# Cross-attention on one core: weights turned on VectorE for TensorE tiles of 32x32, products chained in PSUM, divisions on GpSimd

## The chip, the cores and the metric

The kernel runs on one core of one Trainium2 chip. The metric is the device time of one execution in microseconds (us); lower is better. A core has five engines with a queue each: TensorE (PE, matrix products into PSUM; PEld is its loading of weights), VectorE (DVE), ScalarE (ACT), GpSimd (POOL) and SyncE (SP), which here only issues DMAs. Every engine works through its own queue in order and waits for others by semaphores.

## What is computed

A block of an image model on x of shape (8, 512, 512): a cross-attention with a residual ("x" in the names of the tiles), a self-attention ("a"), a second cross-attention ("c") and an MLP ("m"). All is fp32. The part that matters is the cross-attention, which is there twice. With B = 8, N = 512 rows, H = 512 channels, 16 heads of 32 and a context of S = 77 rows:

```python
q = (xq @ Wq + bq).reshape(B, Lq, nh, dh)
kv = (xkv @ Wkv + bkv).reshape(B, Lkv, 2, nh, dh)
k = kv[:, :, 0]
v = kv[:, :, 1]
scores = jnp.einsum('bqhd,bkhd->bhqk', q, k) / jnp.sqrt(jnp.float32(dh))
attn = jax.nn.softmax(scores, axis=-1)
out = jnp.einsum('bhqk,bkhd->bqhd', attn, v).reshape(B, Lq, H)
return x_q + (out @ Wp + bp)
```

`xq` and `xkv` are layer-normalised (and in the first one modulated) rows of x and of the context.

## The kernel before

`cross_phase` (from L537) runs one cross-attention. Keys `kT` and values `vs` of all batches are made beforehand; `vs` holds the values with the 77 context rows on partitions and is loaded once from DRAM (L394, L466). The loop at L786 has B x KC = 32 rounds, one for each batch `b` and each group `fc` of four heads (128 channels). Four rounds are called a block here.

A round computes the scores of its own group and carries, between them, the rest of the group before (`before`) and a piece of the projections of neighbouring batches:

- `Softmax.scores` (L681): 16 products (L687) of 128 query rows by 77 context rows, contraction 32, four heads side by side in the array. They go to two PSUM tiles `sc[0]`, `sc[1]` of two banks each, from the pool `ps_s` with two such tiles. Half 0 gets its maxima (L703), a subtraction (L704) and one exponential (L714); half 1 gets negated maxima (L710) and eight exponentials of 77 columns (L717) with the maxima as bias.
- `total` (L724) sums the weights, `divide` (L727, L728) takes the reciprocal and multiplies; all on VectorE.
- `turn` (L741) turns the weights of one head with four products by the identity into PSUM; `keep` (L745) copies them to SBUF on ScalarE. There are four pairs a round.
- `outputs` (L751): four products, contraction 77, of 32 channels by 512 rows, in four column tiles of the array; ScalarE reads them with the value bias (L759).
- One `Seven` (L486) in each round in the middle of the stage: seven half-size products (L509) for a 2x2 split of a 512-wide product, for queries (`queries`, L610) or for the output projection (`project`, L641). Each product is two matmuls over K. Products 1, 6, 2, 5, 7, 4, 3 go to halves of PSUM banks of the pool `ps_m`; p1, u2, p5, u3, u4 are the intermediate sums that VectorE, ScalarE and GpSimd make. Queries are made at fc = 0 and 3, projections at fc = 1 and 2.
- `ln_rows` (L251) normalises the rows of a coming batch in pieces, `turned_rows` (L763) turns them with four groups of transposes (L280) and four ScalarE evictions (L284); this is in the round fc = 2. `x_sums` and `o_sums` (L590, L600) make the sums that the seven products need, four GpSimd instructions each.

The order of the instructions on TensorE, VectorE, ScalarE and GpSimd is the order of the Python code, by `manual_schedule`; nothing is reordered. A wait at the head of a queue therefore holds all behind it.

Of the kernel before, what the change touches and what calls it, by code (L numbers as in the profile page):

```python
# [19 lines left out]
P = 128  # L20
# [9 lines left out]
def tile_pixart_block(ctx: ExitStack, tc: tile.TileContext, a: dict, out: bass.AP):  # L30
# [241 lines left out]
    def ln_T(b, nm, pool, psp, res, scale=None, shift=None, tag="t"):  # L272


        xb = x_sb[nm, b]
        xT = res["xT"] = pool.tile([P, KC, N], F32, tag="xnT", bufs=1, name=f"xnT_{nm}{b}")
        for k in range(KC):
            pt = psp.tile([P, H], F32, tag=tag, name=f"lnT_ps_{nm}{b}_{k}")
            for t in range(NT):
                nc.tensor.transpose(pt[:, ts(t, P)], xb[:, t, ts(k, P)], ident)  # L280
            if scale is None:
                nc.scalar.copy(xT[:, k, :], pt)
            else:
                nc.scalar.activation(  # L284
                    xT[:, k, :], pt, AF.Identity,
                    bias=shift[:, k, b : b + 1], scale=scale[:, k, b : b + 1],
                )
            yield
# [49 lines left out]
    with tc.tile_pool(name="ps_s", bufs=2, space=PSUM, reuse_waits="tile") as ps_s:  # L338
# [17 lines left out]
        def context_x(eps, w_k, w_v, bkv, work, prep, cx):  # L356
# [3 lines left out]
            vs = work.tile([S, B, H], F32, tag="cv", bufs=1, name="cv_x")  # L360
# [33 lines left out]
            nc.sync.dma_start(out=vs, in_=vd.rearrange("(b s) h -> s b h", s=S))  # L394
# [13 lines left out]
            return kT, vs, last, mark, mv  # L408

        class ContextC:  # L410
# [42 lines left out]
            def room(self, pool):  # L453
                self.kT = pool.tile([P, KC, R], F32, tag="ckT", bufs=1, name="ckT_c")
                self.vs = pool.tile([S, B, H], F32, tag="cv", bufs=1, name="cv_c")

            def values(self, t):
# [7 lines left out]
                if t == CT - 1:  # L465
                    nc.sync.dma_start(out=self.vs, in_=self.vd.rearrange("(b s) h -> s b h", s=S))  # L466
# [19 lines left out]
        class Seven:  # L486
# [5 lines left out]
            ORDER = (1, 2, 6, 5, 7, 4, 3)  # L492

            def __init__(self, nm, lhs, rhs, work, first, fifth, third, dst, done=None):
                self.nm, self.lhs, self.rhs, self.work = nm, lhs, rhs, work
                self.first, self.fifth, self.third = first, fifth, third
                self.dst, self.done = dst, done

            def temp(self, tag):
                return self.work.tile([P, N2], F32, tag=tag, bufs=1 + (tag != "u3"), name=f"{tag}_{self.nm}")  # L500

            def steps(self):
                add = ALU.add
                for n, i in enumerate(self.ORDER):
                    if n % 2 == 0:
                        bank = ps_m.tile([P, 2, N2], F32, tag="m", name=f"s{n}_ps_{self.nm}")
                    ps = bank[:, n % 2]
                    for k in range(2):
                        nc.tensor.matmul(  # L509
                            ps, lhsT=self.lhs[i][:, k], rhs=self.rhs[i][:, k],  # L510
                            start=(k == 0), stop=(k == 1),
                        )

                    if i == 2:
                        p1 = self.temp("p1")
                        self.first(p1, bank[:, 0])
                        nc.vector.tensor_tensor(self.dst[0, 0], ps, p1, add)
                    elif i == 5:
                        u2, p5 = self.temp("u2"), self.temp("p5")
                        nc.vector.tensor_tensor(u2, bank[:, 0], p1, add)  # L520
                        self.fifth(p5, ps)
                        u4 = self.temp("u4")
                        nc.gpsimd.tensor_tensor(u4, u2, p5, add)
                    elif i == 4:
                        u3 = self.temp("u3")
                        self.third(u3, bank[:, 0], u2)
                        nc.gpsimd.tensor_tensor(self.dst[1, 1], u3, p5, add)
                        nc.vector.tensor_tensor(self.dst[1, 0], ps, u3, add)
                        if self.done is not None:
                            self.done(1)  # L530
                    elif i == 3:
                        nc.vector.tensor_tensor(self.dst[0, 1], ps, u4, add)
                        if self.done is not None:
                            self.done(0)
                    yield

        def cross_phase(  # L537
            nm, eps, w, names, modulated, kT, vs, stack, behind, following, head, fill
# [10 lines left out]
            add, sub = ALU.add, ALU.subtract  # L549

# [3 lines left out]
            def sums(engine, s1, s2, s3, s4, a11, a12, a21, a22):  # L554

                engine.tensor_tensor(s1, a21, a22, add)
                engine.tensor_tensor(s2, s1, a11, sub)
                engine.tensor_tensor(s3, a11, a21, sub)
                engine.tensor_tensor(s4, a12, s2, sub)

            def differences(engine, t1, t2, t3, t4, b11, b12, b21, b22):

                engine.tensor_tensor(t1, b12, b11, sub)
                engine.tensor_tensor(t2, b22, t1, sub)
                engine.tensor_tensor(t3, b22, b12, sub)
                engine.tensor_tensor(t4, b21, t2, sub)
# [4 lines left out]
            sums(  # L571
                nc.gpsimd, *sq,
                w_q[:, low, :H2], w_q[:, high, :H2], w_q[:, low, H2:], w_q[:, high, H2:],
            )
            to = four("to", [P, 2, H2])

            dq = small.tile([P, 2], F32, tag="dq", bufs=1, name=f"dq_{nm}")
            nc.vector.tensor_tensor(dq, bias_cols(bq, 2, 2), bias_cols(bq, 2, 0), sub)


            db = work.tile([P, H2], F32, tag="db", bufs=1, name=f"db_{nm}")
            nc.gpsimd.tensor_tensor(db, bo_row[:, H2:], bo_row[:, :H2], sub)

            def weights_o():
                differences(
                    nc.gpsimd, *to,
                    w_o[:, low, :H2], w_o[:, low, H2:], w_o[:, high, :H2], w_o[:, high, H2:],
                )

            def x_sums(b, engine):  # L590
# [4 lines left out]
                differences(  # L595
# [4 lines left out]
            def o_sums(b, engine):  # L600
# [4 lines left out]
                sums(  # L605
# [4 lines left out]
            def queries(b, j):  # L610
# [7 lines left out]
                for i in range(2):  # L618
# [8 lines left out]
                }  # L627
                return Seven(
                    f"q{nm}{b}_{j}", lhs, rhs, work,

                    lambda p1, ps: nc.scalar.activation(
                        p1, ps, AF.Identity, bias=bias_cols(bq, 1, j)
                    ),
                    lambda p5, ps: nc.scalar.copy(p5, ps),
                    lambda u3, ps, u2: nc.vector.scalar_tensor_tensor(
                        u3, ps, dq[:, j : j + 1], u2, add, add
                    ),
                    {(r, c): qT[r][:, (first, second)[c]] for r in range(2) for c in range(2)},
                ).steps()

            def project(b, j):  # L641
# [16 lines left out]
                def fifth(p5, ps):  # L658
                    nc.scalar.copy(p5, ps)
                    nc.gpsimd.tensor_tensor(p5, p5, db, add)  # L660

                def done(r):
# [6 lines left out]
                    f"o{nm}{b}_{j}", lhs, rhs, work,  # L669
                    lambda p1, ps: nc.vector.tensor_tensor(p1, ps, bo_row[:, :H2], add), fifth,  # L670
                    lambda u3, ps, u2: nc.vector.tensor_tensor(u3, ps, u2, add),
                    {(r, c): res[j + 2 * r][:, ts(c, H2)] for r in range(2) for c in range(2)}, done,
                ).steps()

            class Softmax:


                def __init__(self, b, fc):
                    self.b, self.fc, self.nm = b, fc, f"{nm}{b}_{fc}"

                def scores(self, before):  # L681
                    b, fc = self.b, self.fc
                    qT = st[b]["q"].pop(fc)
                    sc = [ps_s.tile([P, 2, H], F32, tag="s", name=f"s_{self.nm}_{i}") for i in range(2)]
                    for t in range(NT):
# [12 lines left out]
                    self.p = [  # L698
                        work.tile([P, 2, NT, S], F32, tag="p", bufs=4, name=f"p_{self.nm}_{i}")
                        for i in range(2)  # L700
                    ]

                    nc.vector.tensor_reduce(self.mx[0], self.sv[0], AX.X, ALU.max)  # L703
                    nc.vector.tensor_tensor(  # L704
                        self.p[0], self.sv[0], self.mx[0].unsqueeze(3).to_broadcast([P, 2, NT, S]),
                        ALU.subtract,
                    )
                    if before:
                        before.divide(1)
                    nc.vector.tensor_reduce(self.mx[1], self.sv[1], AX.X, ALU.max, negate=True)  # L710

                def exp(self, i, r=0):
                    if i == 0:
                        nc.scalar.activation(self.p[0], self.p[0], AF.Exp)  # L714
                        return
                    for t in range(NT):
                        nc.scalar.activation(  # L717
                            self.p[i][:, r, t, :], self.sv[i][:, r, t, :], AF.Exp,
# [3 lines left out]
                def total(self, i):  # L722
                    self.sm = small.tile([P, 2, NT], F32, tag="sums", name=f"sm_{self.nm}_{i}")
                    return nc.vector.tensor_reduce(self.sm, self.p[i], AX.X, ALU.add)  # L724

                def divide(self, i):
                    nc.vector.reciprocal(self.sm, self.sm)  # L727
                    return nc.vector.tensor_tensor(  # L728
                        self.p[i], self.p[i], self.sm.unsqueeze(3).to_broadcast([P, 2, NT, S]), ALU.mult
                    )  # L730

                def turn(self, h):

                    if h == 0:
                        self.pT = [
                            work.tile([S, 2, H], F32, tag="pT", bufs=2, name=f"pT_{self.nm}_{i}")
                            for i in range(2)
                        ]
# [887 lines left out]
```

## Time and profile before

| | us |
|---|---|
| median of 3 runs | 2536.84 |
| lowest, highest | 2528.83, 2537.41 |
| span of the profiled execution | 2534.4 |
| first scores to the next stage's first transposes, x | 81.6 to 453.4 |
| the same, c | 1364.8 to 1725.1 |

The span is measured from the first to the last instruction of the profiled execution. Busy times in the profile are sums over instructions that can overlap on TensorE; the clock column of a stretch is the share of full speed that TensorE was granted. The page's row of TensorE clock over 40 equal slices:

```profile
PEclk9899999999999999999999999999999999999999
```

Chains of waits give start and length of each piece in us; groups of instructions give the count, the busy time in us and the mean in ns.

### The profile page before, as it was taken

The page shows a single profiled execution, that of the slowest core. Times are in us where ns is not written, and L with a number is a line of the kernel's source. Part 1 is how long each engine was busy: PE and PEld are TensorE (multiplying, and loading weights), DVE is VectorE, ACT ScalarE, POOL GpSimd, SP SyncE. Part 2 cuts the span into 40 slices and gives each one's busy share as a digit, 9 for nine tenths or more (in the row PEclk, how much of TensorE's full clock was granted, in tenths as well). Part 3 has the DMA queues.
Part 4 walks back from the last instruction along what each step waited for, and adds up shares of the span by engine and source line. Part 5 has one row for each costly group of instructions (what it writes and reads, how often), then busy time and mean ns, then how long its engine had stood idle before and what let it go on. Part 6 is the DMA issues. An engine that isn't in the chain of part 4 may idle for free.

```text
span 2534.4 us, 35276 instructions
## 1 busy us (share of the span) xinstructions
PE 2433.2 (96%) x13205; PEld 1561.7 (62%) x13205; DVE 1776.2 (70%) x3230; ACT 1226.2 (48%) x2083; POOL 1087.0 (43%) x982
## 2 busy tenths in 40 slices
PE   7999999889999999999989999998999999999998
PEld 3577776423333333333335777767888888888887
DVE  3588887478889888887756888877556555555553
ACT  1466665377677777777653666662121121121120
POOL 2245452266767777767663454535102102012011
PEclk9899999999999999999999999999999999999999
DMA  7323313498989999999996223133111111001010
GB/s 261 137 51 92 92 26 76 90 180 168 199 171 197 191 181 186 182 188 180 201 200 173 68 39 63 19 81 82 40 32 38 33 39 38 26 29 55 17 38 25
DMA packets 112068, 265.05 MB, mean 105 GB/s; under 512 B 12210, under 2 KB 28674, under 8 KB 111770
## 3 DMA queue, kind: packets, MB, share of 16 engines
q0 software_dynamic: 50976, 159.45, 35.1%
q1 hardware_dynamic: 54981, 91.59, 10.9%
q10 hardware_dynamic: 5941, 11.76, 1.4%
q8 instruction: 104, 1.70, 0.3%
q14 instruction: 66, 0.54, 0.1%
HBM read 226.39 MB, written 44.76 MB: 107 GB/s over the span
## 4 chain that ended last, share of the span: by engine, by line
PE 41%; issue 28%; DVE 15%; DMA 6%; POOL 6%; ACT 3%; POOLq 0%; SPq 0%; ACTq 0%; DVEq 0%
PE s_ps_qx L509 4%; PE s_ps_qc L509 4%; DMA e_a<-mxd_a 4%; DVE mx_a L1005 3%; PE proj_ps_a L301 3%; PE sT_a L985 3%; PE v_ps L301 3%; PE s_ps_ox L509 2%; PE q_ps_a L293 2%; PE s_ps_oc L509 2%; POOL res_m L1535 2%; DVE tu_a L1016 2%; DVE part_a L1017 2%; POOL xr L1536 2%; PE o_ps_a L1065 2%
## 5 line engine op out<-in xcount | busy, mean ns | idle before, releaser
L1535 POOL TENSOR_TENSOR res_m<-res_m,gate_m 128x256 f32<-128x256 f32 x64 | 52.1, 814 | 665.1 <-DVE res_m L1533 665.1
L1039 POOL DMA_DIRECT2D e_a<-mxd_a x256 | 249.8, 2045 | 157.4 <-DMA mxd_a<-mxT_a 138.6
L1048 ACT ACTIVATE e_a<-e_a 128x1024 f32<-128x1024 f32 x256 | 264.8, 1057 | 82.4 <-DMA e_a<-mxd_a 82.2
L1003 ACT COPY e_a<-sT_a 128x1024 f32<-128x1024 f32 x256 | 254.7, 1010 | 100.7 <-DVE mx_a L1005 50.5
L1469 ACT ACTIVATE hT<-hT,bcol 128x512 f32<-128x512 f32 x128 | 91.9, 721 | 237.0 <-DVE hT L1444 228.9
L1055 POOL TENSOR_TENSOR sum_a<-e_a,e_a 128x1024 f32<-128x1024 f32 x64 | 151.0, 2389 | 105.6 <-ACT e_a L1048 105.2
L1055 POOL TENSOR_TENSOR sum_a<-sum_a,e_a 128x1024 f32<-128x1024 f32 x64 | 170.7, 2678 | 3.7 <-ACT e_a L1048 3.6
L1005 DVE TENSOR_TENSOR mx_a<-sT_a,mx_a 128x1024 f32<-128x1024 f32 x128 | 150.8, 1216 | 29.7 <-PE sT_a L985 27.3
L985 PE MATMUL sT_a<-qT_a,kT_a 32*128 32x512 f32 x1024 | 151.6, 646 | 14.0 <-ACT e_a L1003 12.4
L1065 PE MATMUL o_ps_a<-e_a,v 128*32 128x512 f32 x1024 | 146.5, 613 | 9.7 <-ACT e_a L1048 9.7
L1436 PE MATMUL q_ps_h<-x_m,w_L_xcond_W_mlp 128*128 128x256 f32 x512 | 132.1, 381 | 0.0
L1436 PE MATMUL q_ps_h<-xT_m,w_L_xcond_W_mlp 128*128 128x256 f32 x512 | 131.4, 379 | 0.0
L1083 DVE RECIPROCAL rz_a<-z_ps_a 128x512 f32<-128x512 f32 x32 | 107.4, 3357 | 32.0 <-PE z_ps_a L1076 32.0
L293 PE MATMUL q_ps_a<-xnT_a,w_L_xcond_W_qkv 128*128 128x512 f32 x256 | 124.1, 613 | 5.9 <-ACT xnT_a L908 5.9
L1436 PE MATMUL q_ps_h<-x_m,w_s 128*128 128x256 f32 x512 | 122.3, 382 | 5.6 <-DVE w_s L1390 4.9
L293 PE MATMUL k_ps_a<-xnT_a,w_L_xcond_W_qkv 128*128 128x512 f32 x256 | 120.5, 608 | 0.0
L301 PE MATMUL v_ps<-w_L_xcond_W_qkv,xnT_a 128*128 128x512 f32 x256 | 119.7, 611 | 0.0
L301 PE MATMUL proj_ps_a<-w_L_xcond_W_proj,oT_a 128*128 128x512 f32 x256 | 117.9, 604 | 1.4 <-DVE oT_a L1086 1.4
L1436 PE MATMUL q_ps_y<-w_L_xcond_W_mlp,h_s 128*128 128x256 f32 x512 | 113.1, 379 | 0.0
L1436 PE MATMUL q_ps_y<-w_L_xcond_W_mlp,hT 128*128 128x256 f32 x512 | 113.1, 379 | 0.0
L1451 ACT COPY p_h<-q_ps_h 128x256 f32<-128x256 f32 x64 | 23.7, 370 | 183.7 <-PE q_ps_h L1436 183.7
L985 PEld LDWEIGHTS sT_a<-qT_a,kT_a 32*128 32x128 f32 x1024 | 42.0, 183 | 114.4 <-issue 43.4
(368 smaller groups left out, 5609.4 us busy)
## 6 DMA issues: line engine op xcount, KB each, us to landing
e_a<-mxd_a POOLq DMA_DIRECT2D x256, 512.0 KB, 11.7
xa<-res_x POOLq DMA_DIRECT2D x32, 256.0 KB, 5.4
xa<-res_a POOLq DMA_DIRECT2D x32, 256.0 KB, 14.8
x_c<-xa SPq DMA_DIRECT2D x8, 1024.0 KB
w_L_xcond_W_mlp<-in_L_xcond_W_mlp_dram SPq DMA_DIRECT2D x8, 1024.0 KB
xa<-res_c POOLq DMA_DIRECT2D x32, 256.0 KB, 5.2
x_m<-xa SPq DMA_DIRECT2D x8, 1024.0 KB
xr<-xa SPq DMA_DIRECT2D x64, 128.0 KB
```

Of the source, the lines that this page charges most:

```text
L293: nc.tensor.matmul(ps, lhsT=w[:, k, ts(j, P)], rhs=xT[k], start=(k == 0), stop=(k == KC - 1))
L301: nc.tensor.matmul(ps, lhsT=xT[k][:, cols], rhs=w[:, k, :], start=(k == 0), stop=(k == KC - 1))
L509: nc.tensor.matmul(ps, lhsT=self.lhs[i][:, k], rhs=self.rhs[i][:, k], start=(k == 0), stop=(k == 1),)
L985: nc.tensor.matmul(sc[h // 2][:, h % 2, :], lhsT=kT[ts(h, HD), ts(k, P)], rhs=qT[ts(h, HD), :], start=True, stop=True,)
L1003: nc.scalar.copy(self.e[k][i], sc[i])
L1005: nc.vector.tensor_tensor(self.mx[1 - i], sc[1 - i], self.e[0][1 - i] if k == 1 else self.mx[1 - i], ALU.max,)
L1039: nc.gpsimd.dma_start(out=self.e[k][i].rearrange("p h n -> p (h n)"), in_=self.mxd[2 * i : 2 * i + 2, :] .rearrange("h n -> (h n)").partit ...
L1048: nc.scalar.activation(self.e[k][i], self.e[k][i], AF.Exp)
L1055: engine.tensor_tensor(sum_i, self.e[0][i] if k == 1 else sum_i, self.e[k][i], ALU.add)
L1065: nc.tensor.matmul(self.po[ts(h, HD), :], lhsT=vt[:, self.fc * P + h * HD : self.fc * P + (h + 1) * HD], rhs=self.e[k][h // 2][:, h % 2, : ...
L1083: nc.vector.reciprocal(r, self.pz)
L1436: nc.tensor.matmul(self.banks[n][:, half], lhsT=lhsT, rhs=rhs, start=(k == 0), stop=(k == len(pairs) - 1),)
```

## The change

Five things change in `cross_phase` and what it calls.

1. **Turning the weights.** The weights are kept in four fixed tiles `p_half` whose 77 columns are padded to 96 with zeros. `turn` is now two VectorE transposes of 32x32 squares (8 groups x 3 squares each), from SBUF to SBUF; the 16 TensorE turns and the four ScalarE copies are gone.
2. **Outputs in sixteen tiles.** The values of a batch are loaded four times (`load_values`), once for each group of 32 partitions, in squares of 32 context rows. `outputs` is 3 x 4 x 4 products of at most 32 x 32 by 128 columns, one for each square of context rows, head and group of 32 partitions, added up over the three squares. They go to columns 308 to 435 of the four banks that the scores of the round in hand occupy (`now.sc`), and ScalarE reads each half with one instruction.
3. **Chained products.** In a `Seven`, products 1, 6, 5, 3 add up in one PSUM region `a`, which is read after each of them (p1, u2, u4, c12), and 7, 4 add up in a half of `b`. The reads are on ScalarE for queries; for projections p1 and c12 are on VectorE, u2 and u4 on ScalarE with a bias add on GpSimd. A Seven's last two products (3, 4) move into the next round, behind its scores (`pending`).
4. **Divisions.** `divide(0)` goes to GpSimd, `divide(1)` to VectorE where fc is 1 or 2 and to GpSimd where it is 0 or 3.
5. **Placement.** The row turns move from fc = 2 to fc = 0, queries to fc = 1 and 3, projections to fc = 2 and 0, sums for queries to fc = 1 and for projections to fc = 2. The pool `ps_m` has three banks for products and one (two before) for row turns.

```diff
-            pt = psp.tile([P, H], F32, tag=tag, name=f"lnT_ps_{nm}{b}_{k}")
+            pt = psp.tile([P, H], F32, tag=tag, bufs=1, name=f"lnT_ps_{nm}{b}_{k}")
...
+            def product(self, ps, i, first=False):
+                for k in range(2):
+                    nc.tensor.matmul(
+                        ps, lhsT=self.lhs[i][:, k], rhs=self.rhs[i][:, k],
+                        start=(first and k == 0), stop=(k == 1), skip_group_check=not first,
+                    )
...
+            def whole(self):
+                self.mm(1)
+                self.mm(2)
+                self.take("p1")
+                self.mm(6)
+                self.mm(7)
+                self.take("u2")
+                self.mm(5)
+                self.c11()
+                self.take("u4")
+                if self.flush is not None:
+                    self.flush()
+                self.rest()
+
+            def rest(self):
+                self.c22()
+                self.mm(3)
+                self.take("c12")
+                self.mm(4)
+                self.c21()
+                self.stores()
...
+                def taken(what, dst, ps):
+                    bias = bo_row[:, H2:] if what in ("u4", "c12") else bo_row[:, :H2]
+                    if what in ("p1", "c12"):
+                        nc.vector.tensor_tensor(dst, ps, bias, add)
+                    else:
+                        nc.scalar.copy(dst, ps)
+                        later.append(lambda: nc.gpsimd.tensor_tensor(dst, dst, bias, add))
...
-                    pp = ps_m.tile([P, H], F32, tag="t", name=f"pT_ps_{self.nm}_{h}")
-                    for t in range(NT):
-                        nc.tensor.transpose(pp[:S, ts(t, P)], self.p[h // 2][:, h % 2, t, :], ident)
...
+                    to_ = self.pw[:, :, 2 * i : 2 * i + 2, :].rearrange("p k r (t c) -> p (r t) k c", c=SQ)
+                    nc.vector.transpose(to_, self.p[i].rearrange("p g (k c) -> p g k c", c=SQ))
...
+                    for k in range(KB):
+                        n = min(SQ, S - k * SQ)
+                        for h in range(4):
+                            for i in range(QB):
+                                own = slice(i * SQ, i * SQ + n)
+                                nc.tensor.matmul(
+                                    room[i // 2][ts(h, HD), i % 2, at : at + P],
+                                    lhsT=vr[own, k, fc * P + h * HD : fc * P + (h + 1) * HD],
+                                    rhs=self.pw[own, k, h, :],
+                                    start=(k == 0), stop=(k == KB - 1),
+                                )
...
+                    for r in range(2):
+                        nc.scalar.activation(
+                            o[:, 2 * r : 2 * r + 2],
+                            room[r][:, :, at : at + P].rearrange("p i (t c) -> p i t c", c=SQ),
+                            AF.Identity, bias=bias_cols(bkv, 1, KC + fc),
+                        )
```

The body of the new loop, in its order (the choice of `g`, `side`, `turned` by fc is told above; `tail` is the end of the normalisation of the coming rows, in fc = 0; `mm(i)` is a product of this round's Seven or a step of a filling):

```diff
+                now.scores()
+                if pending:
+                    pending.c22()
+                    pending.mm(3)
+                    pending.take("c12")
+                now.maxima(0)
+                now.shift()
+                now.maxima(1)
+                pump(side, 3)
+                if pending:
+                    pending.mm(4)
+                    pending.c21()
+                    pending.stores()
+                now.exp(0)
+                if before:
+                    before.turn(0)
+                    before.turn(1)
+                run(tail)
+                mm(1)
+                if n:
+                    pump(turned)
+                mm(2)
+                if seven:
+                    seven.take("p1")
+                now.exp(1, 0)
+                now.total(0)
+                now.divide(0, nc.gpsimd)
+                run(side)
...
+                mm(6)
...
+                mm(7)
+                now.exp(1, 1)
+                if fc < 3:
+                    pump(stats)
+                if seven:
+                    seven.take("u2")
...
+                last = now.total(1)
+                now.divide(1, nc.vector if fc in (1, 2) else nc.gpsimd)
+                mm(5)
+                if seven:
+                    seven.c11()
+                    seven.take("u4")
+                if before:
+                    before.outputs(now.sc)
+                flush()
...
+                before, pending = now, seven
```

## The prediction

> **What bounds the kernel now.** I read the page's engine line first, then busy time by stretches, then the chain of waits, then the groups of instructions by form.
>
> ```profile
> PE 2433.2 (96%) x13205; PEld 1561.7 (62%) x13205; DVE 1776.2 (70%) x3230; ACT 1226.2 (48%) x2083; POOL 1087.0 (43%) x982
> ```
>
> TensorE is busy for 96% of the span of 2534.4 us. The change touches only the two cross-attention stages (x: about 82 to 453 us, c: about 1365 to 1725 us). Stretches of 40 us in the middle of each; columns: length, PE, PEld, DVE, ACT, POOL busy (instructions), clock, DMA share, GB/s:
>
> ```profile
> 200.00:240.00 40.00, 39.36 (x334) 30.79 (x333) 34.31 (x74) 26.15 (x68) 21.25 (x22) 1.00 0.28 71
> 1520.00:1560.00 40.00, 39.55 (x337) 31.01 (x336) 34.76 (x76) 26.69 (x69) 19.90 (x21) 1.00 0.23 49
> ```
>
> So TensorE has no slack (39.4 of 40 us, full clock), but VectorE follows close behind with 34.3. The chain of waits (start, length, what) shows a round, that is one (b, fc) of the loop:
>
> ```profile
> 216.19 1.06 PE s_x L687 x32
> 217.25 0.59 PE pT_ps_x L741 x4
> 217.85 1.73 PE s_ps_qx L509 x8
> 219.57 0.44 PE pT_ps_x L741 x4
> ...
> 225.21 0.99 PE o_ps_x L751 x8
> 226.20 1.07 PE s_x L687 x32
> ...
> 236.65 1.06 PE s_x L687 x32
> ...
> 249.08 1.06 PE s_x L687 x32
> ```
>
> The scores (L687) start every 10.0 us, 10.45 after the round from 226.20 and 12.43 after the one with the four row turns (L280); four rounds, one block, take 42.9 us (206.18 to 249.08). A round is TensorE alone: scores 1.06, four turns (L741) of 0.44 to 0.59, seven products (L509) of 0.87, outputs (L751) 0.99.
>
> **What goes and what comes.** Durations from the groups by form of the same stage and of self-attention; columns: line, engine, operation, tiles, shape, count, busy us, mean ns, idle before:
>
> ```profile
> L745 ACT COPY pT_x<-pT_ps_x 77x512 f32<-77x512 f32 x60 | 34.9, 582 | 14.8 <-PE pT_ps_x L741 14.8
> L728 DVE TENSOR_TENSOR p_x<-p_x,sm_x 128x616 f32<-128x616 f32 x30 | 25.8, 861 | 1.0
> L704 DVE TENSOR_TENSOR p_x<-s_x,mx_x 128x616 f32<-128x616 f32 x15 | 12.0, 799 | 0.5
> L631 ACT ACTIVATE p_qx<-s_ps_qx,bcol 128x256 f32<-128x256 f32 x8 | 3.8, 473 | 8.8 <-PE s_ps_qx L509 8.8
> L556 POOL TENSOR_TENSOR os_x<-oT_x 128x512 f32<-128x512 f32 x4 | 5.0, 1262 | 4.6 <-ACT oT_x L759 4.6
> L1016 DVE STREAM_TRANSPOSE tu_a<-mx_a 128x512 f32<-128x512 f32 x124 | 87.8, 708 | 3.2
> ```
>
> Removed per round: TensorE's 16 turns, 0.59 + 3 x 0.44 = 1.9 us, on the path; ScalarE's four copies of 0.58 (not on the path); VectorE's divisions, 1.5 of 2 on average (0.86 each).
>
> Added: two VectorE turns of 768 elements. The 512-element row has 0.71; with VectorE's 1.05 ns an element (0.42 us for 256, 0.69 for 512) that is 0.98. Bounds 0.71 and 1.42 (one and two such rows). Divisions of 616 elements on GpSimd: 0.73 for 256 (L523) and 1.26 for 512 give 1.48; bounds 0.73 and 2.39 (the 1024-wide row, L1055). On VectorE the chaining removes two instructions of about 0.42 from a query Seven (five to three) and one from a projection (six to five); ScalarE takes four pieces of 0.47 instead of two.
>
> The outputs become 48 small products, 96 records (the two matmuls of each L509 product stand as x4, so two each) in place of eight. The four last records of an old output group:
>
> ```profile
> 225.59 0.61 PE L751 MATMUL o_ps_x<-pT_x,cv_x 77*32 77x512 f32 x4
> ```
>
> Each lasts 0.592 (the row's least), all four 0.61: they start some 6 ns apart. 96 x 6.7 ns = 0.64; and sixteen tiles side by side stream six passes of 128 columns, 0.11 each by the turns' 0.44 for four, 0.66. With about 0.2 for changing the tiling I take 0.9. Upper bound: the scores' 33 ns a record (1.06 for 32), 3.2; lower 0.66. I am nearer to the former because it is the same operation.
>
> [...]
>
> By this TensorE's own round falls from 10.0 to 1.06 + 6.07 + 0.9 = 8.0. **But three new waits come.**
>
> First, the outputs are written into the score banks of the round in hand, so the next scores wait until ScalarE has read both halves: 0.16 drain (a 128-column record lasts 0.27, the next starts 0.11 later), 0.10 hand-over (226.20 to 226.30, L751 to L759), 0.36 + 0.47 for two reads of 256 columns, 0.05 back: 1.14 us of idle TensorE in every round. Behind the waiting scores stands all of TensorE's queue.
>
> Second, P1+P6+P5+P3 add up in one bank, so products 6, 5, 3 each wait for a read of that bank, and those reads stand in busy queues. In a projection p1 is read by VectorE behind shift, two maxima and two turns: product 6 waits 1.8 us. The projection's c12 stands ahead of the next round's maxima on VectorE and waits for product 3, which follows the scores: the maxima start 1.4 us late. u2 stands on ScalarE behind all the exponentials.
>
> Third, the four row turns have one bank instead of two and their evictions (0.78) are interleaved with the exponentials, after two normalisations (0.82 each) in the same queue.
>
> **The sum.** I walk every queue in the order in which the code issues, with these rows, from the start of a round's scores. *Queries after a projection* (fc 1, 3): c12 at 2.1, maxima 2.5 to 3.3, shift to 4.1, exp(0) 4.2, p1 4.8, eight exponentials 5.1 to 6.8, u2 to 7.25, product 5 to 8.15, outputs to 9.1, plus 1.14: **10.2**. *Projection* (fc 2): VectorE still owes a division and two sums, maximum 1.5; turns 4.1 to 5.9, p1 to 6.3, products 6, 7, 5 to 8.95, outputs to 9.9, plus 1.14: **11.0**. *fc 0*: normalisations end at 4.9, row turns at 5.0, 6.5, 8.0, 9.5, exp(1,1) to 10.2, u2 to 10.6, product 5 to 11.5, outputs to 12.4, plus 1.14: **13.5**. A block: 2 x 10.2 + 11.0 + 13.5 = 45.0. The same walk of the old loop gives 41.9 where the trace shows 42.9 in x and 42.7 in c, so I add 1.0: 46.0 against 42.8, **+3.2 a block**.
>
> Six even blocks in two stages: 12 x 3.2 = +38. Start (first Seven chained before anything can cover it, first block): +2 a stage. End: the rests of one project, turns, outputs and two whole projections, 34 us after the last scores where x has 35.2 (453.4 - 418.2) and c 27.8 (1725.1 - 1697.3); the three rounds before cost about as now: +7 together. Sum +49.
>
> GpSimd is nothing in it: its divisions end by 8.3 us and are wanted at 4 of the next round; at 2.39 the walk doesn't move. If the cover is gone, each late turn costs its own lateness. u4's bias add stands behind a division there in fc 0 and 3; c22, first on VectorE, gets it at 0.2 of the next round, before the scores end. The sums of x and o move to other rounds on GpSimd (four of 1.26) and end within them. The single value load at a stage's start becomes four or more per block on SP, two rounds ahead of use, behind x loads that now issue earlier; SP is otherwise idle. Turns at 0.71 or 1.42 make it -14 or +24.
>
> **Clock.** Idle TensorE has a second price here:
>
> ```profile
> 88.10:91.50 3.40, 1.62 (x17) 0.98 (x16) 3.26 (x9) 1.45 (x6) 0.72 (x1) 1.00 0.00 0
> 91.50:98.40 6.90, 6.44 (x41) 2.65 (x36) 6.21 (x12) 1.30 (x2) 0.73 (x1) 0.51 0.00 0
> ```
>
> With 1.8 of 3.4 us idle the next 6.9 ran at 0.51. The new rounds have 1.1 to 1.8 us gaps a few us apart; in the walk one halved stretch costs 2.9. Only the projections' 1.8 reaches that, where it falls whole into one stretch; of the 14 such rounds of fc 2 I take a third, five: +15. [...]
>
> 2534.4 + 49 + 15 = 2598 for the profiled execution, whose span is 2.4 below the median 2536.8: **2600 us**, 2.5% more.
>
> **Rivals.** *TensorE stays the only bound* (faster): the takes arrive inside the product that covers them. Then a block is 4 x (8.0 + 1.14) + 4 x 0.44 = 38.3, -4.5 x 15 blocks: 2470. For it: VectorE's sum does not grow, ScalarE's falls. Against: queue order, which the walk follows. It decides from when p1 is read within 0.87 us of product 1. *Stalls half as long*: (38.3 + 45.0) / 2 + 1.0 = 42.7, the old block: 2540. *The clock halves in every block* (16 x 2.9): 2630. *Outputs bound by issue*, 3.2 instead of 0.9, 62 rounds: +143, 2740. That the turns stay on TensorE is excluded by the diff.
>
> **Chances.** Forecast 0.50, clock in every block 0.20, issue 0.08, half stalls (no change) 0.08, TensorE only 0.14. This kernel's measurement can't tell less than 0.5% from none. Slower 0.78, same 0.08, faster 0.14. Range 2528 to 2670: it takes in the turns' bounds, the halved clock and the no-change case, and leaves out most of the two far ones. The forecast alone: 2575 to 2630.
>
> **What would show it.** Scores wait about 1.1 us on ScalarE's oT (L759's successor) in each round; projections' product 6 waits on VectorE's p1; blocks take 46 to 49 us; output groups take 0.7 to 0.9; GpSimd divisions about 1.5. I am wrong if blocks are below 42.9, or output groups above 1.5 us.

## The result, and the profile after

The changed kernel takes 2624.84 us (median of 4 runs, 2623.15 to 2628.04) against 2537.12 for the kernel before beside it: ratio 1.0355, 95% interval 1.0335 to 1.0375. It is slower by 88 us; the forecast was 2600 us, 63 more. The profiled execution spans 2622.7 us.

The engine line of the page, then the two stretches of 40 us shown before, of the kernel after (columns as there):

```profile
PE 2409.0 (92%) x17813; PEld 1535.7 (59%) x17813; DVE 1779.5 (68%) x3164; ACT 1152.1 (44%) x1987; POOL 1134.4 (43%) x988
```
```profile
200.00:240.00 40.00, 35.42 (x523) 27.47 (x520) 34.76 (x68) 19.38 (x54) 20.46 (x19) 1.00 0.35 78
1520.00:1560.00 40.00, 33.94 (x606) 25.89 (x605) 31.93 (x63) 17.60 (x52) 22.69 (x21) 1.00 0.37 74
```

TensorE has work for 34 to 35 of 40 us where it had 39.4 and 39.6, at full clock. The groups by form of the changed instructions in the x stage:

```profile
L809 DVE STREAM_TRANSPOSE pw_x<-p_x 128x768 f32<-128x768 f32 x49 | 44.8, 951 | 0.0
L800 POOL TENSOR_TENSOR p_x<-p_x,sm_x 128x616 f32<-128x616 f32 x36 | 43.8, 1223 | 85.0 <-ACT p_x L789 36.2 <-DVE sm_x L796 31.8 <-DVE lnv_x L220 14.3
L821 PE MATMUL s_x<-pw_x,vr_x 32*32 32x128 f32 x1536 | 25.6, 279 | 0.0
L831 ACT ACTIVATE oT_x<-s_x,bcol 128x256 f32<-128x256 f32 x48 | 20.2, 471 | 23.5 <-PE s_x L821 23.5
```

A turn lasts 0.95 us (estimated 0.98), a division on GpSimd 1.22 (1.48), a read of half the outputs 0.47. The timeline of TensorE at the end of a round (start, length, then what ended an idle time before it):

```profile
243.15 1.13 PE L496 MATMUL sa_ps_ox<-to_x,os_x 128*128 128x256 f32 x4 [0.47 <-ACT u_ox L721]
244.21 1.48 PE L821 MATMUL s_x<-pw_x,vr_x 32*32 32x128 f32 x96
246.23 1.48 PE L756 MATMUL s_x<-ckT_x,qT_x 32*128 32x77 f32 x32 [0.53 <-ACT oT_x L831]
```

From the first output to the next scores lie 2.02 us. The scores then last 1.48 instead of 1.13: their first half starts after ScalarE's first read, their second half waits for the second. The waits of TensorE over two blocks, 93.6 us (total, times, longest):

```profile
PE s_x L756 <- ACT oT_x L831: 4.2, 8, 0.5
PE sa_ps_ox L496 <- DVE p_ox L719: 2.2, 2, 1.1
PE sa_ps_qx L496 <- ACT p_qx L692: 1.3, 2, 0.7
PE sb_ps_ox L496 <- DVE res_x L522: 1.1, 2, 0.5
PE sa_ps_ox L496 <- ACT u_ox L721: 0.9, 2, 0.5
PE lnT_ps_x L280 <- ACT x_x L247: 0.7, 2, 0.4
```

Where a block of the x stage goes, worked out by giving each instruction of TensorE the time until the next one starts (206.0 to 253.0 after, 206.2 to 249.1 before):

| us a block | before | after |
|---|---|---|
| turns | 7.3 | 0 |
| outputs, with the wait behind them | 4.0 | 8.1 |
| scores | 4.3 | 5.6 |
| 28 products | 25.0 | 29.7 |
| row turns | 2.4 | 3.4 |
| sum | 42.9 | 46.8 |

And by parts of the run, from the start of the groups (x, then c; "first block" is from the first scores to those four rounds later):

| us | before | after |
|---|---|---|
| start to the first scores of x | 81.6 | 85.3 |
| first block | 48.7, 45.7 | 55.3, 51.6 |
| six later blocks | 257.4, 256.3 | 279.8, 278.8 |
| last three rounds | 30.5, 30.5 | 37.6, 34.4 |
| last scores to the next stage | 35.2, 27.8 | 35.2, 36.2 |
| self-attention, to the first scores of c | 911.4 | 919.8 |

The later blocks hold 45 us of the loss, the edges of the stages 44. Of self-attention's 8.4 us, 7.7 lie behind its end, between c's first row turns and its first scores.

### The profile page after: what moved, and what is told of

Read it like the earlier page. It is cut to its first block, busy times and chain, and to the rows that moved or that the text cites. A ratio compares the mean times of both kernels' runs of the same rounds, so it can differ in the third digit from the quotient of the medians.

```text
span 2622.7 us, 44270 instructions
## 1 busy us (share of the span) xinstructions
PE 2409.0 (92%) x17813; PEld 1535.7 (59%) x17813; DVE 1779.5 (68%) x3164; ACT 1152.1 (44%) x1987; POOL 1134.4 (43%) x988
## 5 line engine op out<-in xcount | busy, mean ns | idle before, releaser
L1082 PE MATMUL sT_a<-qT_a,kT_a 32*128 32x512 f32 x1024 | 149.8, 643 | 12.4 <-ACT e_a L1100 10.6
L800 POOL TENSOR_TENSOR p_x<-p_x,sm_x 128x616 f32<-128x616 f32 x48 | 58.4, 1223 | 148.4 <-DVE sm_x L796 80.1
L800 POOL TENSOR_TENSOR p_c<-p_c,sm_c 128x616 f32<-128x616 f32 x48 | 58.5, 1225 | 133.5 <-DVE sm_c L796 65.9
```

Source lines behind the costliest of these rows:

```text
L800: engine.tensor_tensor(v, v, self.sm[i].unsqueeze(3).to_broadcast([P, 2, NT, S]), ALU.mult)
L1082: nc.tensor.matmul(sc[h // 2][:, h % 2, :], lhsT=kT[ts(h, HD), ts(k, P)], rhs=qT[ts(h, HD), :], start=True, stop=True,)
```

## The experiments

All are edits of the changed kernel unless said otherwise. Times are medians; ratios are to the kernel before, with 95% intervals.

**1. The wait for the outputs' reads (`outputs_early`).**

```diff
+                if before:
+                    before.outputs(now.sc)
                 mm(5)
...
-                if before:
-                    before.outputs(now.sc)
```

> Theory (reads of the outputs in the score banks): between the first output of a round and the first scores of the next lie 2.02 us, 1.22 of them the starts of the 96 records, and the second half of the scores waits another 0.35. With product 5 between the outputs and the next scores both waits (0.8 + 0.35 us a round, 4.6 us a block) are covered; blocks go from 46.8 to about 42.2 us, the time from 2625 to about 2555. Rival (the outputs themselves need the 2.0 us, whatever follows): blocks stay at 46.8 and the time at 2625. Rival (VectorE, busy 37.7 us a block, and the late takes fill the gap): blocks 44 to 45 us, 2590.

2602.9 us, 1.026 (1.025 to 1.028). The outputs' wait is gone, but most blocks fall only to 44.2 to 44.9 (46.2 to 47.5 in the change). The waits of TensorE over two blocks of this kernel:

```profile
PE sa_ps_ox L496 <- DVE p_ox L719: 3.6, 2, 1.8
PE sb_ps_ox L496 <- DVE res_x L522: 3.0, 2, 1.5
```

Of the 4.6 us that were to come off a block about 2.1 do. Of the rest, 1.65 a block are lost at VectorE's reads of the projections (p1, and c22, the quarter of a Seven's result that VectorE sums ahead of product 4): 6.6 us over two blocks where the change had 3.3. The other 0.85 were not traced. Blocks are as the third expectation has them; the time is 13 us above it.

**2. The late takes (`takes_early`), and both together (`both_early`).**

```diff
-                    pending.take("c12")
+                    if pending.done is None:
+                        pending.take("c12")
                 now.maxima(0)
                 now.shift()
+                if pending and pending.done is not None:
+                    pending.take("c12")
...
+                mm(1)
+                if seven:
+                    seven.take("p1")
                 now.exp(0)
...
-                mm(1)
...
-                if seven:
-                    seven.take("p1")
```

> p1 is taken ahead of exp(0) on ScalarE and ahead of the two turns on VectorE, a projection's c12 on VectorE behind the shift instead of ahead of the maxima. Theory (takes late in their queues): the seven products' stretches hold 29.7 us a block against 25.0 before; the 4.7 us shrink to about 1.5, blocks from 46.8 to about 43.6, the first round by 2 us a stage; time about 2575. Rival (the wait only moves on to u2 and product 5, since exponentials start no earlier): blocks 45.5, 2605. Rival (the waits hang on VectorE's amount of work, not on its order): no change, 2625.

> Both edits together. If the two waits are separate and TensorE is left as the bound: 46.8 - 4.6 - 3.2 = 39.0 us a block, 2625 - 70 - 50 = about 2505, below the kernel before. VectorE's 37.7 us a block is the floor. If they share their slack (the outputs' wait gave the late takes their time): blocks 41 to 42 us, 2540 to 2550.

2627.2 us (1.037, 1.034 to 1.039) and 2601.3 (1.025, 1.024 to 1.027): nothing against the change and against `outputs_early`; of the expectations only "no change" for the first was met. In `both_early` the round fc 2 of the later blocks does fall, mostly from 11.2 to 9.35 us against `outputs_early`, and fc 3 rises from 11.05 to between 12.6 and 15.4. Its timelines there, of TensorE, VectorE and GpSimd:

```profile
217.99 1.13 PE L496 MATMUL sa_ps_ox<-w_L_xcond_Wp,os_x 128*128 128x256 f32 x4
222.13 1.67 PE L496 MATMUL sb_ps_ox<-to_x,oT_x 128*128 128x256 f32 x4 [3.00 <-DVE res_x L522]
223.59 1.91 PE L496 MATMUL sa_ps_qx<-xnT_x,w_L_xcond_Wq 128*128 128x256 f32 x4
```
```profile
215.35 1.12 DVE L225 TENSOR_SCALAR lnv_x<-lnv_x 128x4 f32<-128x4 f32 x1
216.38 0.15 DVE L227 TENSOR_TENSOR lnt_x<-lny_x 128x4 f32<-128x4 f32 x1
216.56 1.13 DVE L228 TENSOR_TENSOR lnt_x<-lnt_x,lnv_x 128x4 f32<-128x4 f32 x1
217.72 0.65 DVE L229 SCALAR_TENSOR_TENSOR lny_x<-lnt_x,lny_x 128x4 f32<-128x4 f32 x1
218.30 0.78 DVE L795 TENSOR_REDUCE sm_x<-p_x 128x8 f32<-128x616 f32 x1
...
221.65 0.42 DVE L522 TENSOR_TENSOR res_x<-sb_ps_ox,u_ox 128x256 f32<-128x256 f32 x1
```
```profile
215.22 1.23 POOL L800 TENSOR_TENSOR p_x<-p_x,sm_x 128x616 f32<-128x616 f32 x1 [2.66 <-DVE lnv_x L220]
216.40 1.27 POOL L624 TENSOR_TENSOR os_x<-oT_x,os_x 128x512 f32<-128x512 f32 x1
217.63 1.40 POOL L722 TENSOR_TENSOR u_ox<-u_ox,row_L_xcond_bp 128x256 f32<-128x256 f32 x2
```

Product 4 (222.13) waits 3.0 us for c22 (221.65), which stands in VectorE's queue behind the inverse roots of the row statistics. Three of these, on 128x4 numbers, last 0.65 to 1.13 us instead of 0.16, and each ends 0.02 us after a GpSimd instruction does (at 216.45, 217.67, and for the first of the two adds at L722 at 218.35). So they wait for GpSimd, and behind them VectorE's whole queue does. From 214.99 to 218.30 and from 220.40 to 221.65 the roots hold the queue for 4.6 us; 2.4 of these are stretch, the rest are their own. The products after the gap run at a granted clock of 0.50 (1.67 and 1.91 us instead of 1.03). This was a new theory, tested in 6.

**3. The chain undone (`unchained`), and the turns without the chain (`turns_alone`).** The first gives each product a half bank of its own; sums on VectorE and GpSimd as in the kernel before:

```diff
+                pair = {1: 0, 2: 0, 6: 1, 7: 1, 5: 2, 4: 2, 3: 3}[i]
+                if pair not in self.banks:
+                    self.banks[pair] = ps_m.tile([P, 2, N2], F32, tag="m", name=f"s{pair}_ps_{self.nm}")
...
+                    vadd(self.u2, self.banks[1][:, 0], self.p1, ALU.add)
...
+                    self.fifth(self.p5, self.banks[2][:, 0])
+                    nc.gpsimd.tensor_tensor(self.u4, self.u2, self.p5, ALU.add)
+                    self.third(self.u3, self.banks[1][:, 1], self.u2)
+                    nc.gpsimd.tensor_tensor(self.dst[1, 1], self.u3, self.p5, ALU.add)
```

> The seven products write to halves of banks of their own again and are added up by VectorE and GpSimd as in the kernel before; turns, sixteen-tile outputs, divisions and the order of the loop stay. VectorE gets about 2.5 us a block more (40.2). Theory (the chain in one bank makes the products wait): the 4.7 us of product waits go, blocks from 46.8 to 42 to 43.5 us, time about 2565. Rival (the products wait for late queues, not for the chain): VectorE's added work makes the blocks longer, 47 to 49 us, 2640 to 2660.

The second is the kernel before with the VectorE turns, the sixteen-tile outputs and all divisions on GpSimd:

```diff
-                    if before:
-                        before.divide(1)
...
-                    return nc.vector.tensor_tensor(
+                    return nc.gpsimd.tensor_tensor(
...
                     before.turn(0)
-                    before.keep(0)
+                    before.turn(1)
...
+                if before:
+                    before.outputs(now.sc)
                 next(g, None)
-                if before:
-                    before.outputs()
...
                 last = now.total(1)
+                now.divide(1)
```

> The kernel before with the turns on VectorE, the sixteen-tile outputs one product ahead of the next scores, and all divisions on GpSimd; the seven products stay unchained, as before. Theory (TensorE is relieved by 7.3 us a block of turns and gets about 1 us of longer outputs; VectorE's sum stays near 38 us a block): blocks of 39 to 41 us against 42.9, time 2480 to 2510, so that turns and tiles are a gain and the chain with its order lost it. Rival (VectorE's queue, not TensorE, sets the round as soon as the turns are on it): blocks 43 to 46 us, 2540 to 2590.

2668.4 us (1.053, 1.050 to 1.056) and 2638.3 (1.040, 1.038 to 1.042). Without the chain it is slower both ways, and slower than any expectation: later blocks of 51 to 54 us and of 48 to 51 us in x. The same stretch of `unchained`:

```profile
200.00:240.00 40.00, 34.75 (x485) 28.26 (x484) 32.31 (x67) 14.10 (x42) 22.95 (x24) 0.87 0.32 87
```

The products still wait for VectorE, now for the sums that free their banks (13.5 us in seven waits from 200 to 380 us), and the granted clock of the stretch is 0.87. Undoing the chain gives no time back. What the chain alone costs or saves is not shown: both runs also give VectorE its sums back, both stretch the roots (by 39 and 41 us in all, 31 in the change), and from each stage's first row turns to the next stage's they spend 201 and 116 us at half clock where the change spends 58.

**4. The divisions (`divide_vector`).**

```diff
-                now.divide(0, nc.gpsimd)
+                now.divide(0, nc.vector)
...
-                now.divide(1, nc.vector if fc in (1, 2) else nc.gpsimd)
+                now.divide(1, nc.vector)
```

> The changed kernel with every division on VectorE. If VectorE's queue sets the rounds, six divisions of 0.80 us a block come on top: blocks from 46.8 to 50 to 52 us, 2670 to 2700. If VectorE has room (37.7 of 46.8 us busy) and the prediction's walk is right that where the divisions stand costs nothing: 2620 to 2635.

2658.3 us (1.049, 1.047 to 1.052), most later blocks 49.3 to 50.8: 3 us longer, all of it in fc 2 (14.4 us, 11.0 in the change). Where the divisions stand is not free. VectorE is busy for 37.7 of a block's 47 us in the change, and what is added lasts longer than its own 0.80 us: 37 of the 128 divisions, nearly all in fc 1 and 2, are stretched, by 36 us in all. How much of the 3 us is added work and how much is stretch was not separated.

**5. Other orders (`starts`, `best1`).**

```diff
-            for p in p_half[0] + p_half[1]:
-                nc.gpsimd.memset(p[:, :, S:], 0.0)
...
             queries(0, 0).whole()
+            for p in p_half[0] + p_half[1]:
+                nc.gpsimd.memset(p[:, :, S:], 0.0)
...
-            pump(rows[1], 3)
...
                 now.maxima(1)
+                if n == 0:
+                    pump(rows[1], 3)
...
-                run(tail)
+                if n:
+                    run(tail)
...
                     seven = None
+                    run(tail)
```

> Only the edges of the two stages: the zeroing of the padding columns on GpSimd stands behind the first query product instead of ahead of the sums of the weights, and in the first round the row statistics follow the maxima and the four normalisations follow the products. In the changed kernel the fourth zeroing of the second stage waits 7.0 us for a store of self-attention, with the sums of the weights behind it, and in the first round p1 is taken 8 us late behind four normalisations. Theory: the way from the second stage's first row turns to its first scores goes from 21.1 to about 14 us, the first rounds from 24.4 and 23.0 to about 19; time 2625 - 17 = about 2608. Rival (the row turns with one bank end the first round whatever stands ahead of them): the first rounds keep within 2 us, 2614 to 2618.

`best1` adds the outputs of 1, the queries' p1 ahead of `exp(0)`, and

```diff
-                    pump(stats)
+                    pump(stats, 2 if fc == 0 else 1)
...
-                if fc == 2:
-                    pump(stats)
-                elif fc == 3:
+                if fc == 3:
```

> Outputs ahead of product 5, p1 of the queries ahead of exp(0), the edits of the stages' edges, and the row statistics a round earlier (both halves in the round fc 0, where VectorE idles; the inverse roots in fc 1 and 2 instead of fc 2 alone). If VectorE's queue in fc 1 to 3 sets the block (busy there without a gap, 2.7 us of it in tiny instructions that wait for GpSimd): blocks from 44.7 to about 42.5, and with 17 us from the edges 2603 - 17 - 30 = about 2555. If only the order in the queues counts and not the sum: about 2585.

2628.9 us (1.037, 1.035 to 1.039) and 2621.3 (1.034, 1.032 to 1.036): above every expectation. In `starts` each wait took a new name. The waits of GpSimd and TensorE at the second stage's start in the change:

```profile
POOL p_c L596 <- DMA xa<-res_a: 7.0, 1, 7.0
```
```profile
PE sa_ps_qc L496 <- ACT p_qc L692: 8.6, 1, 8.6
PE lnT_ps_c L280 <- ACT xnT_c L282: 4.1, 6, 0.7
PE sa_ps_qc L496 <- POOL sq_c L620: 3.0, 1, 3.0
```

With the zeroing moved, the sums of the weights themselves waited 8.0 us for the same store: not the place of the zeroing is at fault, but the buffer that each got in its turn (7 gives the sums theirs first, and they don't wait). In the first round p1 was on time, but the roots stood behind the sums of the products, and the row turns, with one bank, took 8 us in c: 25.0 and 24.5 us, no shorter.

In `best1` the roots came beside other GpSimd work. Counting what each instruction of the roots lasts beyond 0.17 us, from the first to the last scores of the two stages, they were stretched by 66 us in all, against 31 in the change, and most fc 2 took 14 to 15 us.

**6. The interference (`roots_moved`, `roots_takes`, `all_gpsimd`).** The roots go where GpSimd is idle; `roots_moved` on top of `outputs_early`, `roots_takes` on top of `both_early`:

```diff
                     before.turn(1)
+                if fc == 3:
+                    pump(stats, 2)
...
-                if fc < 3:
+                if fc < 2:
                     pump(stats)
...
-                if fc == 2:
-                    pump(stats)
-                elif fc == 3:
+                if fc == 3:
```

> outputs_early with the inverse roots of the row statistics (twelve instructions of VectorE on 128x4 numbers) taken from fc 2 to the round fc 3, behind the two turns, where GpSimd stands idle. In outputs_early three or four of these per block last 0.65 to 1.12 us instead of 0.17, each while a GpSimd instruction runs, and VectorE has no gap from fc 1 to fc 3. Theory (this interference is what makes VectorE's queue late in fc 2 and 3): VectorE wins some 2.5 us a block, blocks from 44.7 to 42 to 42.5, time from 2603 to about 2565. Rival (VectorE's sum over the block counts, wherever the roots stand, and they stay as slow elsewhere): 44 to 45 us, 2595 to 2605.

> both_early with the inverse roots moved in the same way. In both_early the round fc 2 fell to 9.35 us and fc 3 rose to 12.6 to 15.2, its product 4 waiting for c22 behind the slow roots on VectorE. Theory: with the roots gone from there fc 3 takes about 10.5, a block 12.4 + 9.4 + 9.4 + 10.5 = 41.7 us, time from 2601 to about 2550. Rival (VectorE is late in fc 3 by its sum, not by the roots): fc 3 stays above 12.5, time above 2590.

2592.2 us (1.022, 1.021 to 1.024) and 2559.2 (1.009, 1.008 to 1.011). On `outputs_early` the move brings 11 us, on `both_early` 42. The roots in `roots_takes`, and TensorE's waits over one of its blocks:

```profile
220.64 0.17 DVE L225 TENSOR_SCALAR lnv_x<-lnv_x 128x4 f32<-128x4 f32 x1
220.72 0.15 DVE L227 TENSOR_TENSOR lnt_x<-lny_x 128x4 f32<-128x4 f32 x1
220.91 0.16 DVE L228 TENSOR_TENSOR lnt_x<-lnt_x,lnv_x 128x4 f32<-128x4 f32 x1
221.10 0.16 DVE L229 SCALAR_TENSOR_TENSOR lny_x<-lnt_x,lny_x 128x4 f32<-128x4 f32 x1
```
```profile
PE lnT_ps_x L280 <- ACT x_x L247: 1.2, 2, 0.8
PE sa_ps_ox L496 <- POOL os_x L624: 0.2, 1, 0.2
```

All last 0.15 to 0.17, and the roots' stretch, 31 us in `both_early`, is gone (0.2 us). fc 3 takes 9.88 and most blocks 41.3 to 42.1: less than the 42.7 to 42.9 of the kernel before. With p1 of the projections still behind the turns (`roots_moved`) the stretch is gone too, 33 us of it, yet most blocks stay at 43.6 to 44.4. So ending the stretch is not enough. Nor is it shown to be what the move is worth: the move takes the roots' own time from ahead of c22 as well, about as much again. Part of the 42 us passes through the clock: TensorE spends 126 us at half clock in `both_early` and 61 in `roots_takes`, which is worth 32 us at most (estimated as half of the 65 between them).

The last one also moves the other divisions:

```diff
-                now.divide(1, nc.vector if fc in (1, 2) else nc.gpsimd)
...
                 flush()
+                now.divide(1, nc.gpsimd)
```

> roots_takes with the second half's division always on GpSimd, behind the bias sums of the projections instead of ahead of them. VectorE loses two divisions of 0.80 us a block. If VectorE's queue still sets fc 2 and fc 3: 1 to 1.5 us a block less than roots_takes, about 2530. If GpSimd's queue takes over (divisions end later than the next round's turns): the same or longer than roots_takes, 2550 to 2570.

2558.5 us (1.008, 1.006 to 1.010): the same as `roots_takes`. fc 3 falls to 9.3, fc 1 rises from 9.4 to 10.6, where product 6 waits up to 1.0 us for GpSimd's sums.

**7. The edges (`edges_too`),** on top of `roots_takes`:

```diff
             to = four("to", [P, 2, H2])
+            SQ = 32
...
+            p_half = [
...
+            pump(rows[1], 2)
             queries(0, 0).whole()
+            for p in p_half[0] + p_half[1]:
+                nc.gpsimd.memset(p[:, :, S:], 0.0)
...
-            pump(rows[1], 3)
...
                 now.maxima(1)
+                if n == 0:
+                    pump(rows[1], 2)
...
-                    pump(stats, 2)
+                    pump(stats, 4)
                 if n == 0:
+                    run(tail)
                     seven.rest()
...
+                tag = "m" if b < 2 else "t"
```

> roots_takes with its edges mended. The sums of the query weights get their buffers ahead of the padded halves (so that, as in the kernel before, they need no buffer of a store of self-attention that has not landed) and the zeroing follows the first queries; the statistics of the second block's rows stand ahead of the first queries, their inverse roots behind the first maxima, their normalisations behind the exponentials and the last take; the row turns of the first two blocks use the three banks of the products; all four normalisations of the later blocks stand at the end of fc 3 instead of two of them in fc 0. Theory (each edge is lost to queue order and buffers, which these edits mend): the second stage's start 7 us less, the first rounds from 25 to about 17 us each, fc 0 from 13.3 to about 12.4: 2559 - 7 - 16 - 10 = about 2526, at or just below the kernel before. Rival (as with the edits of the run called starts, the waits only change their names): 2550 to 2560.

**2507.9 us, ratio 0.989 (0.9875 to 0.9908): 1.1% faster than the kernel before.** The two stretches, and TensorE's waits over one block:

```profile
200.00:240.00 40.00, 39.50 (x640) 29.69 (x639) 34.79 (x76) 23.15 (x64) 24.64 (x22) 1.00 0.43 101
1520.00:1560.00 40.00, 39.59 (x643) 30.07 (x641) 35.24 (x76) 22.87 (x66) 24.62 (x22) 1.00 0.36 75
```
```profile
PE sa_ps_ox L498 <- POOL os_x L613: 0.2, 1, 0.2
```

TensorE is the bound again, with VectorE at 35 of 40 us. Later blocks take 39.8 to 41.1 us, first rounds 15.0 and 12.0 (25.5 and 24.7), the way from c's first row turns to its first scores 13.6 (21.3), fc 0 11.7 and 11.2 (13.3 and 12.8). The edits were not tried one by one; only their places separate them.

## Why the prediction was right, and where it was off

The direction and the mechanism (TensorE is relieved, and gives it back in waits) held; the sum was 25 us short. That it came so near is partly luck: the blocks were 7 us short and the edges 33, and the 15 us for a clock that halves in the projections, where it did not, hid part of that. By its terms:

| term | forecast | measured |
|---|---|---|
| twelve later blocks | +38 | +45 |
| starts, with the first blocks | +4 | +24.5 |
| ends | +7 | +19.4 |
| clock | +15 | in the edges |
| MLP | 0 | -0.5 |

- **Outputs.** From first to last start 1.22 us, not 0.9: sixteen tiles start 13 ns apart on average, not the 6.7 taken from the row of four. No run shows the 0.2 for changing the tiling by itself, an estimate of the author's; the trace shows the 1.22 as a whole. The wait behind them, forecast at 1.14, is 0.80 before the scores and 0.35 inside them. The sum is right to 0.01. Experiment 1 took it for a cost that comes off in full, and got back 22 of 70 us.
- **Rounds.** fc 0 to 3 were walked at 13.5, 10.2, 11.0 and 10.2 and measure 13.7, 10.9, 11.0 and 11.2. The query rounds were short by the 0.3 of the outputs, which delays all that follows, and in fc 3 by c22, for which product 4 waits 0.53: u4's bias sum is done at 221.26, but c22 stands behind the roots until 223.89. The other c22 does wait for its bias sum, 1.78, as the walk had seen, and no product waits for it.
- **Late takes.** p1 of the projections is late, and product 6 waits (1.1 us instead of 1.8). But "p1 behind the turns" was no price that can be taken off: with p1 in front, c22 was late instead (experiment 2). Until the roots were moved, fc 2 and 3 together took 22 to 25 us with either order.
- **"GpSimd is nothing in it"** is the step that failed. It was priced by when its divisions are wanted. What its divisions, sums for the products and bias sums also did was to hold VectorE, and the walk priced no VectorE instruction by its neighbour. The effect was there beforehand: in the kernel before, two of the three adds at L228 in a block already last 0.59 and 0.70. The groups of the x stage, L228 in the kernel before, L228 in the change, and L225 in the change (one block; before, it lasts 0.17):

```profile
L228 DVE TENSOR_TENSOR lnt_x<-lnt_x,lnv_x 128x4 f32<-128x4 f32 x15 | 7.3, 485 | 0.5
L228 DVE TENSOR_TENSOR lnt_x<-lnt_x,lnv_x 128x4 f32<-128x4 f32 x15 | 7.2, 483 | 0.5
L225 DVE TENSOR_SCALAR lnv_x<-lnv_x 128x4 f32<-128x4 f32 x1 | 1.1, 1118 | 0.0
```

Roots and divisions on VectorE were stretched by 20 us in all before and by 35 in the change. So the change adds about 1 us a block of it. Moving the roots is worth 11 us, or 42 with the early takes.
- **Edges.** "+2 a stage" and "+7" were hardly worked out. Sums of weights late by a shifted buffer (+7.7), p1 late behind four normalisations (8.6), row turns through one bank and chained products with nothing to cover them are what the traces show there; the whole is +44, and the shares were not measured one by one.
- **Clock.** The forecast put it into the projections. That a third of their rounds would halve it, at 2.9 us each, was the author's estimate, which no run shows: product 6 waits 1.1 us there, and the granted clock stays at 1.00 from 158 to 451 us and from 1493 to 1769. It is halved (0.50) at starts and ends and for 3.4 us in each second block: 58 us from the stages' first row turns to the next stage's, against 31 before, worth 14 us at most (estimated as half of the 27 between them), nearly all inside the 44.

Of the rivals, "TensorE stays the only bound" is what the kernel comes near to once queues are in order (`edges_too`), though at blocks of 39.8 to 41.1, not 38.3, and with VectorE busy for 35 of 40 us. "Outputs bound by issue" is excluded by the 1.22 us. What stays open is how much of the changed kernel's own 45 us is interference: moving the roots alone in it, without the early outputs, was not tried, and no run ends the stretch and leaves the roots where they are.

## What to carry to other kernels

When work moves from one engine to another, walk the queue of the engine that is nearly full, and count what its neighbour does to its instructions (here 0.16 us became up to 1.13), not their durations alone. A wait that is taken away and gives nothing may have a second one right behind it, as here in VectorE's queue (3.0 us at c22 in `both_early`): undo both before you judge either. And read the first round and the start of a stage apart from its middle; here they held 44 of the 88 us.

## What the runs showed of the hardware

- **VectorE held by GpSimd.** Three of the inverse roots' instructions on VectorE (128x4 numbers) lasted 0.65 to 1.13 us beside GpSimd instructions in the lines of `both_early` and 0.16 or 0.17 in those of `roots_takes`; each of the three ended 0.02 us after GpSimd's, and so did 38 of the 41 stretched roots and divisions of the change (0.02 to 0.04). In `divide_vector` 37 of 128 divisions on VectorE were stretched, by 36 us in all, up to 3.36 us where the median is 0.80. Turns and reductions beside GpSimd kept their time (0.93 to 0.97 and 0.74 to 0.79 in the change). Why they end with GpSimd's was not shown.
- **Clock.** In `both_early` one idle time of 3.0 us was followed by 3.4 us at a granted clock of 0.50 (222.6 to 226.0), with products of 1.67 and 1.91 us instead of 1.03.
- **Sixteen tiles** of 32x32 started 96 records in 1.22 us in the change.
